# A two-layer graph network: order of the work inside a share, and a later load of the features

## The chip, the cores and the metric

The kernel runs on one core of a Trainium2 chip, as one launch. The metric is the device time of that launch in microseconds (us). A core has five engines with a queue each: TensorE (PE, matmuls), VectorE (DVE), ScalarE (ACT), GpSimd (POOL) and SyncE (SP). In this kernel SP issues the plain DMAs and POOL the indirect ones (gathers and scatters by a list of indices). Each queue is worked off in its order: an instruction that waits for a semaphore holds what stands behind it.

## The reference

There are 16 graphs (batches) of N = 1024 nodes with C = 64 features each; `adj` is a 0/1 matrix, symmetric, with about 16 neighbours in a row; every node is valid.

```
adj_d = dilate(adj, mask)                 # rows with over 10 neighbours drop every skip-th of them, symmetrically
agg   = weighted sum of the 0.25, 0.5 and 0.75 quantiles, per feature, over the neighbours kept
y     = relu((x + agg) @ W1 + b1) @ W2 + b2
x1    = layernorm(x + y * mask)           # layer 1
msg   = adj @ x1
out   = layernorm(x1 + tanh([x1, msg] @ W1' + b1') @ W2' + b2')    # layer 2
```

The quantiles need, for each node and feature, the sorted values of some 9 to 40 neighbours.

## The kernel before, in words

The batches are taken in five groups of 2, 4, 4, 4 and 2 (`GROUPS`). A group goes through four kinds of work.

**Preparation** (`prepare`, which runs `list_batch` for each batch, L610 to L714). For each half of a batch it loads four adjacency tiles `a` of 128 x 1024 (L620, three buffers), clears the diagonal (L621), loads the tile's features into the last columns of the tile `nb` (L623), turns the adjacency into 0/1 in the first columns of `nb` (L624) and counts it on ACT (L628). A second loop over the same four tiles transposes `nb` (L650, on PE), ranks the neighbours with matmuls (L656, L658) and marks those to drop (L660, L662). Then the kept neighbours of all eight tiles are computed back into `nb` (`p_val`, L670 to L675), the nodes are ordered by their number of neighbours (`places`, L681 to L704), and eight indirect DMAs on POOL scatter the eight tiles `nb`, neighbours and features in one row, into the DRAM tensor `order` (L708). `nb` has nine buffers (`held`, NT + 1), so that a new batch's tile needs a buffer whose scatter has landed.

**Fetch** (`Chunk.fill`, `ChunkByPE.fill`). A group's ordered nodes are cut into chunks of like degree: 9 or 10 for a group, 48 in all. For most chunks DVE finds the positions of the neighbours (MAX8, L817) and POOL gathers one neighbour's features a DMA (L837) into `slots_a` (three buffers). For the others, "by PE", the values come from matmuls with one-hot matrices `hot` that DVE makes (L976, L984), copied to `slots_a` by ACT (L995). Both put the nodes' own features there or into `x_n` first (L826, L925), and pads by ACT copies (L831).

**Selection** (`Chunk.select`). DVE runs a network of min and max over the slots (L873), ACT and PE weight the selected places (L895, L897), then come the first layer's matmuls and its layer norm (L544 to L552, of which ACT does the squares, L548), and the result goes to DRAM (`keep`, L853 or L1002).

**Second layer** (`finish_group`, which runs `messages` for each batch, L1013 to L1054). POOL gathers `x1` back into the order of the nodes (L1017); the adjacency is loaded again (L1025, the same three buffers `a`), transposed on PE (L1030) and copied by ACT (L1031); then come message matmuls (L1040) and the final layer norm.

The main loop (from L1091) runs over steps `s`, one for each chunk. The work of a step is handed out in 24 equal shares (`SHARES`): each kind of work is a Python generator wrapped in `Side`, and `advance` runs it on until its portion of the share is given out. `beside` lists the sides of a step: `fills` of chunk s + 1 (the second half of it) and of chunk s + 2 (the first half), `select` of chunk s, then `going` (the second layer of the group before) and `coming` (the preparation of the next group). At a group's first fetch, what is left of `coming` is drained in one piece. Steps before 0 hand out fills alone; the second layer of the last group is given out after the loop.

Waits, buffers and the final order of each engine's instructions come from the tile framework, which is given the written order. The order in the trace departs from the written one where an instruction was expected to be ready sooner.

Of the kernel before, what the change touches and what calls it, by code (L numbers as in the profile page):

```python
# [9 lines left out]
F32 = mybir.dt.float32  # L10
# [10 lines left out]
P = 128  # L21
# [395 lines left out]
def kernel(  # L417
# [15 lines left out]
    nc = tc.nc  # L433
# [5 lines left out]
    XCOL = N + 2 * INFO  # L439
# [170 lines left out]
    def list_batch(g, b):  # L610

        nbs, gone = [], []
        for half_b in range(2):
            at = slice(b * NT + half_b * HT, b * NT + (half_b + 1) * HT)

            m = rows.tile([P, 2, HT], F32, name="m")
            for t in range(half_b * HT, (half_b + 1) * HT):
                blk = slice(t * P, (t + 1) * P)
                a = rows.tile([P, N], F32, name="a", bufs=3)
                nc.sync.dma_start(a, adj[b, blk, :])  # L620
                nc.vector.tensor_mul(a[:, blk], a[:, blk], off_diag_f)  # L621
                nb = held.tile([P, ROW], BF16, name="nb")
                nc.sync.dma_start(nb[:, XCOL:].bitcast(F32), x[b, blk, :])  # L623
                nc.vector.tensor_scalar(nb[:, :N], a, 0.0, None, op0=ALU.is_gt)  # L624
                r = held.tile([P, N], BF16, name="gone", bufs=NT)
                for h in range(2):
                    cols = slice(h * HALF, (h + 1) * HALF)
                    nc.scalar.activation(r[:, cols], nb[:, cols], AF.Copy,  # L628
                                         accum_out=m[:, h, t - half_b * HT:t - half_b * HT + 1])
                nbs.append(nb)  # L630
                gone.append(r)
                yield


            s = rows.tile([P, 5, HT], F32, name="s")
            skip, do, want, biases = s[:, 0], s[:, 1], s[:, 2], (s[:, 3], s[:, 4])
            mh = halves[:, at]
            nc.vector.tensor_add(mh, m[:, 0], m[:, 1])
            nc.vector.tensor_scalar(mh, mh, 0.5, 0.25, op0=ALU.mult, op1=ALU.add)
            nc.vector.tensor_scalar(skip, mh, ROUND, -ROUND, op0=ALU.add, op1=ALU.add)  # L640
            nc.vector.scalar_tensor_tensor(do, mh, 0.5 * T_THRESH + 0.25, mask[:, at],
                                           op0=ALU.is_gt, op1=ALU.mult)
            nc.vector.scalar_tensor_tensor(want, skip, 1.0, do, op0=ALU.add, op1=ALU.mult)
            nc.vector.tensor_scalar(biases[0], skip, -3.0, -2.0 * FAR, op0=ALU.mult, op1=ALU.add)
            nc.vector.scalar_tensor_tensor(biases[1], m[:, 0], 2.0, biases[0], op0=ALU.mult, op1=ALU.add)
            for t in range(half_b * HT, (half_b + 1) * HT):
                nb, r, col = nbs[t], gone[t], slice(t - half_b * HT, t - half_b * HT + 1)
                p = ps_t.tile([P, N], BF16, name="p_nb", tag="tr")
                for j in range(NT):
                    nc.tensor.transpose(p[:, j * P:(j + 1) * P], nb[:, j * P:(j + 1) * P], ident_h)  # L650
                nb_t = rows.tile([P, N], BF16, name="nb_t")
                nc.scalar.copy(nb_t, p)  # L652

                for h in range(2):
                    p = ps_m.tile([P, HALF], F32, name="p_rank", tag="rv", bufs=3)
                    nc.tensor.matmul(p, far_h, nb[:, h * HALF:(h + 1) * HALF], start=True, stop=False)  # L656
                    for c in range(HT):
                        nc.tensor.matmul(p[:, c * P:], nb_t[:, (h * HT + c) * P:(h * HT + c + 1) * P],  # L658
                                         reach[:, :HALF - c * P], start=False, stop=c == HT - 1)
                    nc.scalar.activation(r[:, h * HALF:(h + 1) * HALF], p, AF.Abs,  # L660
                                         bias=biases[h][:, col], scale=2.0)
                nc.vector.tensor_scalar(r, r, 1.0, want[:, col], op0=ALU.add, op1=ALU.is_equal)  # L662
                yield
        count = work.tile([P, 2, NT], F32, name="count")
        for t in range(NT):
            blk = slice(t * P, (t + 1) * P)
            for h in range(2):
                cols = slice(h * HALF, (h + 1) * HALF)
                p = ps_m.tile([P, HALF], F32, name="p_val", tag="rv", bufs=3)
                nc.tensor.matmul(p, ident_h, nbs[t][:, cols], start=True, stop=False)  # L670
                nc.tensor.matmul(p, minus_h, gone[t][:, cols], start=False, stop=False)
                for j in range(HT):
                    nc.tensor.matmul(p[:, j * P:(j + 1) * P], gone[h * HT + j][:, blk], minus_h,
                                     start=False, stop=j == HT - 1)
                nc.scalar.activation(nbs[t][:, cols], p, AF.Relu, accum_out=count[:, h, t:t + 1])  # L675
            yield

        mine = work.tile([P, NT, INFO], F32, name="mine")
        nc.scalar.copy(mine[:, :, 1], mask[:, b * NT:(b + 1) * NT])
        deg = mine[:, :, 0]  # L680
        nc.vector.scalar_tensor_tensor(deg, count[:, 0], 1.0, count[:, 1], op0=ALU.add, op1=ALU.add)  # L681
        low = work.tile([P, NT], F32, name="low", bufs=1)
        nc.vector.tensor_scalar(low, deg, float(BINS - 1), None, op0=ALU.min)
        own = work.tile([P, NT, BINS], BF16, name="own", bufs=1)
        nc.vector.tensor_tensor(own, bins[:, None, :].to_broadcast([P, NT, BINS]), bcast(low, BINS),
                                op=ALU.is_equal)
        p = ps_m.tile([P, 512], F32, name="p_tot", tag="m")
        for t in range(NT):
            nc.tensor.matmul(p[:, :BINS], ones_h, own[:, t], start=t == 0, stop=t == NT - 1)
        base = work.tile([P, BINS + 1], F32, name="base", bufs=1)  # L690
        nc.vector.memset(base[:, 0:1], 0.0)
        nc.vector.tensor_tensor_scan(base[:, 1:], ones_h[:, :BINS], p[:, :BINS], 0.0, op0=ALU.mult, op1=ALU.add)
        p = ps_m.tile([P, NT, BINS], F32, name="p_at", tag="m")
        nc.tensor.matmul(p, ident, base[:, None, :BINS].to_broadcast([P, NT, BINS]), start=True, stop=False)
        for t in range(NT - 1):
            nc.tensor.matmul(p[:, t + 1:], ones_h, own[:, t:t + 1].to_broadcast([P, NT - 1 - t, BINS]),
                             start=False, stop=False)
        nc.tensor.matmul(p, above, own, start=False, stop=True)
        hit = work.tile([P, NT, BINS], F32, name="at_hit", tag="wide", bufs=1)
        nc.vector.tensor_mul(hit, p, own)  # L700
        at = work.tile([P, NT], F32, name="at", bufs=1)
        nc.vector.tensor_reduce(at, hit, AX.X, ALU.add)
        at_i = places[:, b * NT:(b + 1) * NT]
        nc.vector.tensor_copy(at_i, at)  # L704
        moves = []
        for t in range(NT):
            nc.vector.tensor_copy(nbs[t][:, N:XCOL].bitcast(F32), mine[:, t])
            move = nc.gpsimd.indirect_dma_start(  # L708
                out=g.order[b - g.b0], out_offset=bass.IndirectOffsetOnAxis(ap=at_i[:, t:t + 1], axis=0),
                in_=nbs[t].bitcast(I32), in_offset=None)  # L710
            for other in moves:
                tc.declare_no_dep(move.ins, other.ins, reason="the places of all nodes differ")
            moves.append(move)
        yield  # L714
# [378 lines left out]
    coming = start(0)  # L1093
    coming_of, going = 0, None
    fills = {}
    for s in range(-LEAD, len(plan)):
        j = s + LEAD
        if j < len(plan):
            i, (k, t0, t1, by_pe) = plan[j]
            if coming is not None and i == coming_of:  # L1100
                coming.drain()
                coming = start(i + 1) if i + 1 < len(GROUPS) else None
# [5 lines left out]
        beside = []  # L1108
# [5 lines left out]
        select = None  # L1114
        if s + 1 < len(plan) and (s < 0 or plan[s][0] != plan[s + 1][0]) and s + 1 >= 0:
            weigh_group(groups[plan[s + 1][0]])
        if s >= 0:
            i = plan[s][0]

            if s > 1 and plan[s - 1][0] == i != plan[s - 2][0] and i:  # L1120
                if going is not None:
                    going.drain()
                going = Side(finish_group(groups[i - 1]), groups[i - 1].count * (NT + NT // QT + 1))
            select = Side(chunks[s].select(), chunks[s].select_count())
# [4 lines left out]
            if coming is not None:  # L1129
                beside.append((coming, weight[min(s + LEAD, len(plan) - 1)] / sum(  # L1130
                    w for w, (q, _) in zip(weight, plan) if q == coming_of - 1)))
        for _ in range(SHARES):
            for side, share in beside:
                side.advance(share / SHARES)
# [220 lines left out]
```

## Time and profile before

| | |
|---|---|
| median of 3 runs | 3105.35 us (3076.01, 3105.35, 3121.26) |
| the profiled execution | 3108.18 us, span 3106.3 us |
| granted TensorE clock, mean | 0.891 |
| instructions | 65,859 |
| L837, fetches on POOL | 1012, 1412.1 us busy, mean 1395 ns |
| L873, selection on DVE, the three costliest groups of it | 355.4, 284.8 and 197.1 us |
| L984, `p_slots` on PE | 12,288 matmuls, 710.8 us, mean 270 ns |
| L976, `hot` on DVE | 456, 310.8 us, mean 697 ns |
| DMA | 264.06 MB, mean 85 GB/s |

The busy time of an engine leaves out waits, DMA issues and semaphore instructions. A list of waits says which instruction's engine stood idle before it, which instruction or DMA it waited for, for how long in total, how often and how long at most. "SPq" is SP's queue of DMA issues. "issue" stands for a time in which the engine waited for nothing that the profile shows. A timeline gives the start, the duration and the instruction, with the idle time before it and what ended it in brackets. The time of a DMA instruction on SP or POOL is that of its issue; the data land later.

### The profile page before, as it was taken

What the parts mean: (1) busy time and instruction counts of PE and PEld (TensorE: products, weight loads), DVE (VectorE), ACT (ScalarE), POOL (GpSimd) and SP (SyncE); (2) the same over time, 40 slices, a digit from 0 to 9 for tenths busy, and PEclk for the clock granted to TensorE, in tenths of its full rate; (3) what the DMA queues carried; (4) which work ended last, traced back from release to release, by engine and by line L of the source; (5) the groups of instructions that cost most, each with busy time, mean ns of one, the idle gap of its engine ahead of it and who ended that gap; (6) DMA issues with size and microseconds to landing.
All of it is one profiled execution on the core that took longest, in us unless ns stands there. A gap on an engine that the chain in (4) does not pass through costs nothing. (4 is left out here: it accounts for less than half of the span.)

```text
span 3106.3 us, 65859 instructions
## 1 busy us (share of the span) xinstructions
PE 2404.8 (77%) x25076; PEld 1875.9 (60%) x25076; DVE 2385.0 (77%) x5434; ACT 1593.3 (51%) x4047; POOL 1735.7 (56%) x1511
## 2 busy tenths in 40 slices
PE   5447847778577989885788999876868996689977
PEld 2245635466465777574566787664757875567755
DVE  3359957579579998997698978995898888967731
ACT  5615636646154656752356656633445455335553
POOL 3174762156856386638588465657552756646410
PEclk9769978889788999897899999997989998889988
DMA  2420332323132424241332424312421232122222
GB/s 96 146 76 24 113 105 92 104 59 113 41 119 55 122 57 121 67 127 40 105 82 75 135 72 122 97 43 56 125 82 50 70 102 76 43 68 80 70 87 80
DMA packets 223571, 264.06 MB, mean 85 GB/s; under 512 B 149683, under 2 KB 150290, under 8 KB 223248
## 3 DMA queue, kind: packets, MB, share of 16 engines
q1 hardware_dynamic: 176528, 189.18, 20.7%
q0 software_dynamic: 46720, 70.61, 8.8%
q8 instruction: 198, 3.24, 0.4%
q14 instruction: 125, 1.02, 0.1%
HBM read 218.07 MB, written 46.27 MB: 85 GB/s over the span
## 5 line engine op out<-in xcount | busy, mean ns | idle before, releaser
L837 POOL DMA_INDIRECT slots_a<-in_x_dram,idx x1012 | 1412.1, 1395 | 815.1 <-issue 270.9
L984 PE MATMUL p_slots<-hot,parts 128*64 128x256 bf16 (+1 forms) x12288 | 710.8, 270 | 182.3 <-DVE hot L976 156.5
L984 PEld LDWEIGHTS <-parts 128*64 128x64 bf16 x12288 | 636.7, 114 | 228.6 <-issue 109.8
L873 DVE TENSOR_TENSOR slots_b<-slots_a 128x256 f32<-128x256 f32 (+14 forms) x582 | 355.4, 627 | 101.9 <-DMA slots_a<-in_x_dram,idx 46.6
L1040 PE MATMUL p_msg<-adj_t,x_n 128*64 128x128 f32 x2048 | 281.3, 289 | 59.6 <-DMA x_n<-x,places 33.1
L976 DVE TENSOR_SCALAR hot<-val 128x2048 bf16<-128x2048 bf16 x456 | 310.8, 697 | 16.7 <-PE p_slots L984 8.9
L708 POOL DMA_INDIRECT order<-nb,places x128 | 149.6, 1169 | 307.8 <-issue 293.8
L897 PE MATMUL p_g<-ident,terms 128*64 128x128 f32 x1988 | 272.6, 288 | 30.1 <-ACT terms L895 29.4
L1040 PEld LDWEIGHTS p_msg<-adj_t,x_n 128*64 128x64 f32 x2048 | 233.2, 143 | 92.7 <-DMA x_n<-x,places 42.7
L873 DVE TENSOR_TENSOR slots_a<-slots_b 128x256 f32<-128x256 f32 (+11 forms) x526 | 284.8, 554 | 0.7
L995 ACT COPY slots_a<-p_slots 128x512 f32<-128x512 f32 (+2 forms) x136 | 73.2, 538 | 400.3 <-PE p_slots L984 288.1
L897 PEld LDWEIGHTS p_g<-ident,terms 128*64 128x64 f32 x1988 | 231.9, 144 | 57.4 <-ACT terms L895 47.4
L628 ACT ACTIVATE gone<-nb 128x512 bf16<-128x512 bf16 x256 | 159.8, 627 | 205.1 <-DVE nb L624 204.0
L1017 POOL DMA_INDIRECT x_n<-x,places x128 | 150.6, 1177 | 176.7 <-DMA x<-y 84.2
L658 PE MATMUL p_rank<-reach,nb_t 128*128 128x512 bf16 (+3 forms) x1024 | 191.0, 322 | 53.1 <-ACT nb_t L652 51.9
L1030 PE MATMUL p_adj<-ident,a 128*128 128x128 f32 x1024 | 185.0, 296 | 48.8 <-DMA a<-in_adj_dram 26.6
L817 DVE MAX8 key<-code 128x8 f16<-128x1024 f16 x170 | 207.2, 1219 | 1.7
L658 PEld LDWEIGHTS <-nb_t 128*128 128x128 bf16 x1024 | 95.7, 104 | 178.6 <-ACT nb_t L652 91.3
L873 DVE TENSOR_TENSOR slots_b<-slots_b 128x256 f32<-128x256 f32 (+11 forms) x310 | 197.1, 636 | 0.6
L660 ACT ACTIVATE gone<-p_rank,s 128x512 bf16<-128x512 f32 x256 | 164.5, 685 | 56.7 <-PE p_rank L658 37.2
L624 DVE TENSOR_SCALAR nb<-a 128x1024 bf16<-128x1024 f32 x128 | 88.5, 692 | 132.7 <-DMA order<-nb,places 132.1
L1031 ACT COPY adj_t<-p_adj 128x512 f32<-128x512 f32 x256 | 149.1, 583 | 73.9 <-PE p_adj L1030 71.7
(184 smaller groups left out, 4551.2 us busy)
## 6 DMA issues: line engine op xcount, KB each, us to landing
a<-in_adj_dram SPq DMA_DIRECT2D x256, 512.0 KB
row_p<-order SPq DMA_DIRECT2D x64, 256.0 KB
slots_a<-in_x_dram,idx POOLq DMA_INDIRECT x1012
row<-order SPq DMA_DIRECT2D x192, 64.0 KB
nb<-in_x_dram SPq DMA_DIRECT2D x128, 32.0 KB
row<-order SPq DMA_DIRECT2D x32, 128.0 KB
x_s<-in_x_dram SPq DMA_DIRECT2D x16, 256.0 KB
out_dram<-x_n SPq DMA_DIRECT2D x16, 256.0 KB
```

The source lines that it names most:

```text
L628: nc.scalar.activation(r[:, cols], nb[:, cols], AF.Copy, accum_out=m[:, h, t - half_b * HT:t - half_b * HT + 1])
L658: nc.tensor.matmul(p[:, c * P:], nb_t[:, (h * HT + c) * P:(h * HT + c + 1) * P], reach[:, :HALF - c * P], start=False, stop=c == HT - 1)
L660: nc.scalar.activation(r[:, h * HALF:(h + 1) * HALF], p, AF.Abs, bias=biases[h][:, col], scale=2.0)
L817: nc.vector.max(key[:, t, r:r + 8], code)
L837: nc.gpsimd.indirect_dma_start(out=self.a[:, at[k], t, :], out_offset=None, in_=x_rows, in_offset=bass.IndirectOffsetOnAxis(ap=idx[:, t, k ...
L873: nc.vector.tensor_tensor(view(rb, ra, [(d[0], d[1 + side]) for d in dims]), view(ab, aa, [(d[0], d[1]) for d in dims]), view(bb, ba, [(d[ ...
L897: nc.tensor.matmul(p[:C, col], terms[:, i], ident, start=False, stop=t == e - 1 and first + i == places - 1)
L976: nc.vector.tensor_scalar(hot[:, :, :, e], val, float(inside[at]), None, op0=ALU.is_equal)
L984: nc.tensor.matmul(p[i * C:(i + 1) * C, o:o + w], g.parts[2 * q + i][:, c, h], hot[:, c, i, :w], start=c == 0 and h == 0, stop=c == NT - 1 ...
L1017: nc.gpsimd.indirect_dma_start(out=x1[:, t], out_offset=None, in_=g.x1[b - g.b0], in_offset=bass.IndirectOffsetOnAxis(ap=places[:, b * NT ...
L1030: nc.tensor.transpose(p[:, j, :], a[:, col:col + P], ident)
L1040: nc.tensor.matmul(p[C:2 * C, :QUART], x1[:, j, :], adj_t[:, j, :], start=(j == 0), stop=(j == NT - 1))
```

## The change

Two edits.

The load of a tile's features into `nb` moves within `list_batch` from the first loop over the four tiles of a half (between the load of `a` and the 0/1 adjacency) to the top of the second loop over the same tiles. It is the same DMA, of the same rows, into the same columns, on the same queue.

The list `beside` is sorted, once for each step, before its shares are handed out: first `going` and `coming`, then `select`, then the two `fills`. The sort is stable, so that within each of these the order stays. The portions of each side and the drains stay as they are.

```diff
@@ list_batch, first loop
                 nc.sync.dma_start(a, adj[b, blk, :])
                 nc.vector.tensor_mul(a[:, blk], a[:, blk], off_diag_f)
                 nb = held.tile([P, ROW], BF16, name="nb")
-                nc.sync.dma_start(nb[:, XCOL:].bitcast(F32), x[b, blk, :])
                 nc.vector.tensor_scalar(nb[:, :N], a, 0.0, None, op0=ALU.is_gt)
@@ list_batch, second loop
             for t in range(half_b * HT, (half_b + 1) * HT):
                 nb, r, col = nbs[t], gone[t], slice(t - half_b * HT, t - half_b * HT + 1)
+                nc.sync.dma_start(nb[:, XCOL:].bitcast(F32), x[b, t * P:(t + 1) * P, :])
                 p = ps_t.tile([P, N], BF16, name="p_nb", tag="tr")
@@ main loop
+        beside.sort(key=lambda b: (b[0] is not going and b[0] is not coming, b[0] is not select))
         for _ in range(SHARES):
             for side, share in beside:
                 side.advance(share / SHARES)
```

## The prediction

> **What bounds the kernel now.** I read the page first, for the balance of the engines:
>
> ```profile
> PE 2404.8 (77%) x25076; PEld 1875.9 (60%) x25076; DVE 2385.0 (77%) x5434; ACT 1593.3 (51%) x4047; POOL 1735.7 (56%) x1511
> ```
>
> TensorE and VectorE are each busy for 77%, so neither is the bound by itself; each loses about 700 us, and an order of work is worth what it takes out of those losses. The chain of waits on the page names only the code after the last batch and says nothing of the stages. The windows by stage do:
>
> ```profile
> 130.00:480.00 350.00, 211.92 (x2335) 161.30 (x2337) 265.04 (x735) 149.67 (x375) 209.93 (x150) 0.80 0.30 85
> 480.00:600.00 120.00, 97.64 (x863) 63.15 (x859) 65.77 (x180) 83.38 (x221) 26.42 (x24) 0.89 0.34 106
> 600.00:1500.00 900.00, 696.41 (x7652) 540.91 (x7651) 761.85 (x1679) 471.26 (x1198) 568.51 (x407) 0.88 0.30 84
> 3000.00:3106.00 106.00, 83.84 (x545) 63.57 (x545) 15.12 (x29) 44.16 (x107) 14.29 (x16) 0.91 0.30 93
> ```
>
> Columns: stretch, length, then busy time of PE, weight loads, DVE, ACT, POOL. From 600 to 1500 us DVE is busy for 85%; its idle time lies in the start, in 480 to 600 (the rest of group 1's preparation, given out in one piece: the shares of steps 0 to 5 hold weights 32+38+30+36+26+10 = 172 of group 0's 269, so 36% is drained) and after 3000 (the second layer of the last group, given out after the loop). None of these three is ordered by shares, so the new order can't help there.
>
> Next the waits, of the SP queue and of DVE:
>
> ```profile
> SPq L1025 <- PE p_adj L1030: 367.7, 69, 36.3
> SPq L623 <- DMA order<-nb,places: 366.5, 75, 39.4
> DVE nb L624 <- DMA order<-nb,places: 132.1, 31, 30.1
> DVE a L621 <- DMA a<-in_adj_dram: 65.3, 34, 8.6
> DVE slots_b L873 <- DMA slots_a<-in_x_dram,idx: 46.6, 5, 26.9
> ```
>
> (us in total, times, longest.) SP stands 366.5 us before the feature load of L623, for a buffer `nb` that the scatter of the batch before still reads. DVE waits for the same scatters itself at L624, which the change leaves as it is. The timelines of the turn at 860 us, POOL, SP and DVE, show how it hangs together:
>
> ```profile
> 845.78 1.00 POOL L837 DMA_INDIRECT slots_a<-in_x_dram,idx  x1 [0.31 <-issue]
> 847.08 0.96 POOL L1017 DMA_INDIRECT x_n<-x,places  x1 [0.30 <-issue]
> ...
> 857.10 1.01 POOL L708 DMA_INDIRECT order<-nb,places  x1 [0.30 <-DMA x_n<-x,places]
> ```
>
> ```profile
> 818.86 1.71 SPq L853 DMA_DIRECT2D x<-y  x4
> 860.06 10.21 SPq L623 DMA_DIRECT2D nb<-in_x_dram  x7
> 870.38 0.38 SPq L620 DMA_DIRECT2D a<-in_adj_dram  x1
> ```
>
> ```profile
> 860.01 0.69 DVE L624 TENSOR_SCALAR nb<-a 128x1024 bf16<-128x1024 f32 x1 [15.41 <-DMA order<-nb,places]
> ...
> 874.13 0.29 DVE L621 TENSOR_TENSOR a<-a,off_diag_f 128x128 f32<-128x128 f32 x1 [6.54 <-DMA a<-in_adj_dram]
> ```
>
> The batch's `places` were done at 836.2 (DVE timeline), but POOL first works off fetches, then eight gathers of the second layer, and only at 857.1 the scatters. DVE stands 15.4 us. Then SP hands out seven feature loads at the pace of the scatters, and the adjacency load behind them leaves at 870.4 instead of about 860.7, when L624 had freed its buffer: DVE stands another 6.5 us. The same sequence shows at 410, 1507 and 2151; the four turns cost DVE 30.9+15.8+14.3+29.1 = 90.1 us at L624.
>
> **What the Trainium skill says.** "DMA: Bandwidth & Descriptors", section "Anatomy of one DMA — SWDGE (gpsimd) path", says that DMA engines do not wait on semaphores, the issuing sequencer does, and that some 2 us of such a DMA are fixed, mostly the write receipt. The trace agrees with the first (SP's 39.4 us before one load), and nearly with the second: from the scatter's start at 857.10 to L624 at 860.01 are 2.9 us. "SBUF — State Buffer", section "SBUF: two separate sides", says that POOL can't write descriptors while DVE holds the shared port in a fast mode. A fetch at 840.12 took 5.35 us (median of the line 1.07) while DVE ran `hot` and `select`; this fits and isn't proof. So POOL's pace may move with DVE's order, which I can't price.
>
> **The change, part by part.** Nothing is added or removed: 128 feature loads, 1245 SP issues, 1268 indirect DMAs stay. A step between two stores of `y` takes (2996.6 - 289.4)/47 = 57.6 us, so a share is 57.6/24 = 2.4 us: nothing moves by more than about a share in written order.
>
> *Does written order count?* Only among instructions that are ready. In the tile view of `slots_a`:
>
> ```profile
> L831 ACT COPY slots_a<-big x214: 227/251/486, 30.5 to 2914.7; 128x64 f32<-128x64 f32 x65, 128x192 f32<-128x192 f32 x27, 128x128 f32<-128x128 f32 x12, 128x320 f32<-128x320 f32 x3
> L826 SPq DMA_DIRECT2D slots_a<-order x92: 313/427/1125, 91.3 to 2911.2; - x92
> ```
>
> L831 is written after L826, yet starts 61 us ahead: instructions are laid out by when they were expected to be ready, and written order breaks ties. That limits both edits.
>
> *Feature loads.* 128 x (0.34 + 0.05) us = 50 us of SP time stay on SP. A load needs only a free buffer, and may well be laid out as early as before: then nothing changes. At best every late adjacency load goes: 65.3 us at L621 less 4.0 in the first 60 us = 61. No loss of note: the 340 ns slot only moves past `a`, `row` and `x<-y` on SP, and the scatter that reads the features follows eight tiles of `p_val` later. I take a quarter, -15 us.
>
> *Preparation and second layer first.* On POOL the scatters (L708) and gathers (L1017) pass the fetches of their share: 1012 fetches over 48 x 24 shares are 0.88, each (1412.1 + 270.9)/1012 = 1.66 us, so 1.5 us, at most 2.4, per turn. Over 14 turns that is 20 to 34 us earlier, on DVE's path where it waited: I take -20. On DVE L621, L624 and L662 pass `hot`, MAX8 and `select`; an L624 placed a share earlier before a scatter that is late anyway stands longer, at worst 14 x 2.4 = 34 us. I take +5. What is queued behind it on DVE is the `select` of L873, and PE waits for `hot`.
>
> *Fetches last.* They are delayed by what is given out before them in their share. `select` waits for fetches in 5 places, 46.6 us; a share more each is 12 us, and it can't be below zero as the queue only gets fuller ahead of them; but if all 48 steps came to wait, 48 x 2.4 = 115 us. `hot` (L976, a fetch in the PE variant) is waited for by PE 52 times, 156.5 us; that can move either way by 52 x 2.4 = 125 us at the very most, and mostly other PE work fills in: 0. I take +0 for `hot`, +0 for steps that have slack, and the turns' small loss above stands for both.
>
> Sum: -15 - 20 + 5 = -30 us. The profiled execution took 3108.2 (span 3106.3, 2 us around it), the median of three is 3105.4 (3076.0 to 3121.3), so the profiled one is as good as the median: 3075.
>
> **The rivals.**
> *A, as summed (chance 0.42):* 3075, own range 3040 to 3115. That the feature loads don't move at all lies in it (3090).
>
> *B, faster (0.34):* the turns open up. If the scatters pass not one share's fetches but the whole run in front of them (13 after 833 us at the turn above; 27 in a row before the scatters of 437), two thirds of the 90.1 us at L624 go, 60, and with SP free two thirds of the 61 at L621, 41: 3105 - 101 = 3004. For it: POOL is 56% busy, so it could well serve them earlier. Against: the scatters look to have been laid out for a time at which POOL was expected to be done with the fetches, and then rank is no matter. What is late next is DVE's wait for ACT's squares (L549, 126.6 us), which stays.
>
> *C, slower (0.24):* the fetch of the next chunk becomes the bound. It used to be handed out first in each share, so it had the rest of the share as slack before the first `select`; now it comes last. Add to that POOL's queue: a scatter ahead of fetches holds them while it waits (L708 already stands 293.8 us on POOL). If two thirds of the 48 steps pay a share, 77 us: 3182. It decides from the point at which the waits of L873 for `slots_a` pass about 80 us, from 46.6.
>
> **How the numbers follow.** A measurement of this kernel can tell about 2%, some 62 us (the three runs before differ by 45). Faster by over 2% means under 3043: most of B (0.31) and a little of A (0.05), 0.36. Slower means over 3167: most of C (0.20) and a rest, 0.21. Within 2%: 0.43. The likeliest is A, so 3075. For 8 in 10 the range reaches to the middle of B and past that of C: 2975 to 3190.
>
> **What would show it.** Right: SP's wait at L623's load (now in the second loop) falls from 366.5 us to under 100, with part of it coming back at L620 for a buffer of `a`; L621's 65.3 falls by a quarter or more; L624's 132.1 falls by about 20; L873's wait for fetches rises by 5 to 15; the windows before 130, 480 to 600 and after 3000 stay within a few us. If SP's wait for the scatters stays near 366, the features are laid out as before and that part is nothing. The sum is wrong if L624's wait falls by half or more (B), if L873's wait for fetches or PE's for `hot` rises by over 30 us (C), or if waits that I left at zero, L549's for ACT above all, move by tens of us because the layout comes out different everywhere.

## The result, and the profile after

The changed kernel took 3064.89 us (median of four, 3051.81 to 3070.3) beside 3107.37 for the kernel before (3076.01 to 3121.26): a ratio of 0.9878, 95% interval 0.9831 to 0.9925. Its profiled execution spans 3068.3 us, 38.0 less than the one before. Measured again in the second series below it came to 0.9846 [0.982, 0.9872]. A ratio leaves out executions that took over 1.5% longer than the fastest of the same kernel.

The balance of the engines on the page after:

```profile
PE 2410.6 (79%) x25076; PEld 1897.4 (62%) x25076; DVE 2383.7 (78%) x5434; ACT 1594.5 (52%) x4047; POOL 1737.3 (57%) x1511
```

The counts of instructions and DVE's 2384 us of work are those of before, so the gain is idle time alone. The list of waits after (us in total, times, longest), with the features' load now on L647 and the 0/1 step on L623:

```profile
ACT gone L627 <- DVE nb L623: 213.8, 55, 37.7
ACT node_t L1042 <- PE p_msg L1040: 177.0, 99, 9.1
DVE nb L623 <- DMA order<-nb,places: 151.5, 32, 36.9
...
DVE ln_st L549 <- ACT ln_sq L548: 80.3, 35, 12.5
...
DVE a L621 <- DMA a<-in_adj_dram: 52.0, 31, 7.4
...
PE p_msg L1040 <- ACT adj_t L1031: 38.2, 3, 35.7
...
DVE slots_b L873 <- DMA slots_a<-in_x_dram,idx: 34.7, 3, 24.8
...
PE p_msg L1040 <- DMA x_n<-x,places: 7.6, 8, 1.9
...
PE p_x L1036 <- DMA x_n<-x,places: 1.7, 1, 1.7
```

and four lines of the list of before that the prediction had not shown:

```profile
ACT node_t L1042 <- PE p_msg L1040: 193.7, 102, 27.5
...
DVE ln_st L549 <- ACT ln_sq L548: 126.6, 34, 26.0
...
PE p_msg L1040 <- DMA x_n<-x,places: 33.1, 24, 16.8
...
PE p_x L1036 <- DMA x_n<-x,places: 20.4, 2, 18.6
```

The wait for the scatters, for which the prediction saw a fall, rose from 132.1 to 151.5 us (138.4 in the repeat, `e5_full_again`). What fell is a wait that it had left at zero: DVE's for ACT's squares at L549, by 46.3, and with it PE's waits for gathered rows `x_n`, from 53.5 to 9.3. The longest of each (26.0, 16.8, 18.6, and 27.5 on ACT) shrank too: a few long stops went, not many short ones.

SP, in its own list of the kernel after:

```profile
SPq L647 <- DMA order<-nb,places: 330.8, 45, 50.3
...
SPq L620 <- DVE nb L623: 59.3, 33, 10.0
```

SP still stands 330.8 us at the feature load (366.5 before). DVE's work in the stage of group 1's drained preparation and at the end is as it was (the windows after give DVE 67.39 us busy from 480 to 600, 65.77 before, and 15.13 in the last 106 us, 15.12 before).

**Where the 38 us are.** DVE's stops of over 10 us add up to 292.6 us before and 254.7 after, a difference of 37.9, as much as the span lost. In the repeat they add up to 241.4, 51.2 less than before, and its span is 49.8 shorter. All of the 37.9 lies at the four turns from one group to the next:

| stops of DVE at the turn (us) | before | after | the changed kernel again |
|---|---|---|---|
| first, from 404 to 410 | 30.2 (L624) | 11.0 | 10.9 |
| second, from 791 to 802 | 23.7 (L549) and 15.4 (L624) | 24.1 (L623) | 24.2 |
| third, from 1431 to 1453 | 26.0 (L549) and 14.1 (L624) | 36.9 (L623) | 24.1 |
| fourth, from 2089 to 2151 | 29.1 (L624) | 28.6 | 27.3 |
| sum | 138.5 | 100.6 | 86.5 |

At the second and third turn two stops became one. The timeline of the kernel before shows how the first of such a pair came about (start, duration, engine and instruction; in brackets the idle time before it and what ended that):

```profile
789.66 0.22 DVE L546 TENSOR_TENSOR y<-y,ln_st 128x64 f32<-128x64 f32 x1
...
794.96 0.99 POOL L837 DMA_INDIRECT slots_a<-in_x_dram,idx  x1 [0.30 <-issue]
796.26 0.96 POOL L1017 DMA_INDIRECT x_n<-x,places  x1 [0.31 <-issue]
...
798.84 0.69 PE L1040 MATMUL p_msg<-adj_t,x_n 128*64 128x128 f32 x2 [16.83 <-DMA x_n<-x,places]
...
801.28 0.94 POOL L1017 DMA_INDIRECT x_n<-x,places  x1 [0.30 <-issue]
802.53 1.01 POOL L837 DMA_INDIRECT slots_a<-in_x_dram,idx  x1 [0.30 <-issue]
...
804.40 0.26 ACT L1042 COPY node_t<-p_msg 64x128 f32<-64x128 f32 x1 [27.52 <-PE p_msg L1040]
...
814.44 0.25 ACT L548 ACTIVATE ln_sq<-y 128x64 f32<-128x64 f32 x1
...
814.72 0.22 DVE L549 TENSOR_REDUCE ln_st<-ln_sq 128x1 f32<-128x64 f32 x1 [23.70 <-ACT ln_sq L548]
```

POOL had given out three gathers of the second layer at 722 to 725 us, then 33 fetches, and came to the next five gathers at 796.26. PE stood 16.8 us before the message matmuls for the first of these; ACT stood 27.5 for the message to copy; the squares of a layer norm of *selection*, whose input `y` DVE had finished at 789.9, stood behind that copy on ACT's queue, and behind 10 us of other ACT work that came next on it (some of it waiting for PE in its turn); DVE stood 23.7 for the squares. While POOL was busy with fetches, the gathers behind them held PE, ACT and DVE one after the other, and the wait list puts it down to ACT.

After the change, the same place:

```profile
812.85 1.00 POOL L837 DMA_INDIRECT slots_a<-in_x_dram,idx  x1 [0.30 <-issue]
814.15 0.96 POOL L1017 DMA_INDIRECT x_n<-x,places  x1 [0.30 <-DMA slots_a<-in_x_dram,idx]
...
820.41 1.01 POOL L708 DMA_INDIRECT order<-nb,places  x1 [0.30 <-DMA x_n<-x,places]
...
823.33 0.69 DVE L623 TENSOR_SCALAR nb<-a 128x1024 bf16<-128x1024 f32 x1 [24.06 <-DMA order<-nb,places]
823.44 0.35 SPq L647 DMA_DIRECT2D nb<-in_x_dram  x1
824.05 0.33 SPq L620 DMA_DIRECT2D a<-in_adj_dram  x1
```

Eleven gathers ran from 692.44 us on, ahead of all fetches; PE no longer stands. Then 62 fetches follow in one run, five gathers, and only then the scatters, and DVE stands 24.1 us for them. The scatters left at 857.1 before and leave at 820.4 now, yet DVE reaches them earlier too, so its wait for them grew. The adjacency load behind the feature load leaves 0.6 us after it, where it took 10 us before: seven features no longer stand ahead of it.

At the third turn of the changed kernel a chain runs the other way, and it is the longest stop left: DVE stands 36.9 us at L623 for the scatters, ACT stands 37.7 at L627 for DVE's 0/1 tile, the adjacency copy of L1031 comes behind that on ACT's queue, and PE stands 35.7 at L1040 for the copy.

### The profile page after: what moved, and what is told of

The parts are those of the page before. It is cut to its first block, busy times and chain, and to the rows that moved or that the text cites. A ratio compares the mean times of both kernels' runs of the same rounds, so it can differ in the third digit from the quotient of the medians.

```text
span 3068.3 us, 65888 instructions
## 1 busy us (share of the span) xinstructions
PE 2410.6 (79%) x25076; PEld 1897.4 (62%) x25076; DVE 2383.7 (78%) x5434; ACT 1594.5 (52%) x4047; POOL 1737.3 (57%) x1511
## 5 line engine op out<-in xcount | busy, mean ns | idle before, releaser
L837 POOL DMA_INDIRECT slots_a<-in_x_dram,idx x1012 | 1383.5, 1367 | 762.3 <-issue 287.1
L984 PE MATMUL p_slots<-hot,parts 128*64 128x256 bf16 (+1 forms) x12288 | 720.5, 273 | 145.2 <-DVE hot L976 135.1
L984 PEld LDWEIGHTS <-parts 128*64 128x64 bf16 x12288 | 649.2, 115 | 193.1 <-issue 130.9
L873 DVE TENSOR_TENSOR slots_b<-slots_a 128x256 f32<-128x256 f32 (+14 forms) x582 | 355.1, 628 | 91.4 <-ACT terms L895 37.1
L1040 PE MATMUL p_msg<-adj_t,x_n 128*64 128x128 f32 x2048 | 281.9, 292 | 61.3 <-ACT adj_t L1031 38.2
L708 POOL DMA_INDIRECT order<-nb,places x128 | 158.6, 1239 | 292.1 <-issue 257.7
L1040 PEld LDWEIGHTS p_msg<-adj_t,x_n 128*64 128x64 f32 x2048 | 239.4, 146 | 88.6 <-ACT adj_t L1031 39.1
L1017 POOL DMA_INDIRECT x_n<-x,places x128 | 171.7, 1342 | 205.9 <-DMA x<-y 85.5
L873 DVE TENSOR_TENSOR slots_a<-slots_b 128x256 f32<-128x256 f32 (+11 forms) x526 | 286.0, 556 | 0.7
L627 ACT ACTIVATE gone<-nb 128x512 bf16<-128x512 bf16 x256 | 160.0, 629 | 214.3 <-DVE nb L623 213.8
L1030 PE MATMUL p_adj<-ident,a 128*128 128x128 f32 x1024 | 186.0, 298 | 30.2 <-ACT adj_t L1031 16.4
L623 DVE TENSOR_SCALAR nb<-a 128x1024 bf16<-128x1024 f32 x128 | 88.8, 695 | 152.1 <-DMA order<-nb,places 151.5
L873 DVE TENSOR_TENSOR slots_b<-slots_b 128x256 f32<-128x256 f32 (+11 forms) x310 | 197.6, 638 | 0.5
L660 ACT ACTIVATE gone<-p_rank,s 128x512 bf16<-128x512 f32 x256 | 165.6, 685 | 48.3 <-PE p_rank L658 33.1
L1031 ACT COPY adj_t<-p_adj 128x512 f32<-128x512 f32 x256 | 148.9, 582 | 74.5 <-PE p_adj L1030 71.9
```

Of the source, the lines that this page charges most:

```text
L627: nc.scalar.activation(r[:, cols], nb[:, cols], AF.Copy, accum_out=m[:, h, t - half_b * HT:t - half_b * HT + 1])
L837: nc.gpsimd.indirect_dma_start(out=self.a[:, at[k], t, :], out_offset=None, in_=x_rows, in_offset=bass.IndirectOffsetOnAxis(ap=idx[:, t, k ...
L873: nc.vector.tensor_tensor(view(rb, ra, [(d[0], d[1 + side]) for d in dims]), view(ab, aa, [(d[0], d[1]) for d in dims]), view(bb, ba, [(d[ ...
L984: nc.tensor.matmul(p[i * C:(i + 1) * C, o:o + w], g.parts[2 * q + i][:, c, h], hot[:, c, i, :w], start=c == 0 and h == 0, stop=c == NT - 1 ...
L1017: nc.gpsimd.indirect_dma_start(out=x1[:, t], out_offset=None, in_=g.x1[b - g.b0], in_offset=bass.IndirectOffsetOnAxis(ap=places[:, b * NT ...
L1030: nc.tensor.transpose(p[:, j, :], a[:, col:col + P], ident)
```

## The experiments

The theory from the two traces is the chain above: gathers of the second layer that stood behind a run of fetches cost the time, and the sort let them pass. Its rivals: the features' later load did it through SP; it was the scatters of the preparation that passed fetches, as the prediction had it; or any change of order lands a layout that is faster or slower by chance. The expectations name these as they were called at the time: R (order by readiness, with the gain in the sort) and then G (the gathers) for the theory, F for the features, S for the preparation or the selection, P and L for chance.

All are edits of the kernel before. Each series ran on one chip. Two series fell on chips on which the kernel before took 3877.74 and 3885.52 us at a granted TensorE clock of 0.81; the second ran on one like that of the result (3108.22 us, 0.89). Ratios are taken within a series, and absolute times are compared there only.

### First series (clock 0.81): the two parts, and the order turned round

The features alone (`e1_features_only`: the two lines of the diff in `list_batch`), the sort alone (`e2_order_only`), and two other orders:

```diff
# e3_fetch_before_select: fetches ahead of selection, second layer and preparation still first
+        beside.sort(key=lambda b: (b[0] is not going and b[0] is not coming, b[0] is select))
# e4_select_first: selection, fetches, then second layer and preparation
+        beside.sort(key=lambda b: (b[0] is going or b[0] is coming, b[0] is not select))
```

> Only the move of the feature load; the shares are handed out as before. Theory R (instructions are laid out by readiness; a feature load needs only a free buffer, so the move is worth little, and the sort gives the gain): ratio to before 0.993 to 1.003, SP's wait for the scatters at the feature load stays over 250 us. Rival F (the feature load held SP, and its move gives the gain): ratio 0.983 to 0.991, DVE's wait for adjacency at L621 falls from 65 us to about 50. Theory P (any change of the written order lays the work out anew, and the time moves by up to 1% either way without a cause in the edit): anything from 0.985 to 1.015.

> Only the sort of the shares (second layer and preparation, then selection, then fetches); the feature load stays in the first loop. Theory R: ratio 0.984 to 0.992, nearly all of the gain, and DVE's wait for ACT's squares at L549 falls from 127 us to about 80 as in the changed kernel. Rival F: 0.996 to 1.004. Theory P: anything from 0.985 to 1.015, and not the sum that e1 and the full change would give.

> Feature load in the first loop; second layer and preparation first, then the fetches, then selection. Tells which half of the sort matters. If the gain lies in putting second layer and preparation first: as e2, ratio 0.984 to 0.993. If it lies in selection ahead of the fetches (the squares of its layer norm pass the ACT copies of the fetch by PE): 0.996 to 1.004, with L549's wait near 127 us. Theory P: anything from 0.985 to 1.015.

> Feature load in the first loop; selection first, then the fetches, then second layer and preparation. The other half of the sort alone. If the gain lies in selection ahead of the fetches: ratio 0.984 to 0.993 and L549's wait near 80 us. If it lies in second layer and preparation first: 0.996 to 1.004. Theory P: anything from 0.985 to 1.015.

Measured: 0.9992 [0.995, 1.0035], 0.998 [0.9953, 1.0006], 0.9982 [0.9956, 1.0009] and 1.0113 [1.0054, 1.0173]. On this chip neither part is worth anything that can be told; e2 so misses the 0.984 to 0.992 of theory R. Giving selection and fetches ahead of the rest costs about 1%, of which the clock may be a third: e4's executions had a mean of 0.8065 beside 0.8124, and a straight line through those of the kernel before that the ratio counts falls by 27.5 us for 0.01, an estimate of 16 of the 44 us. The list of waits of e1 shows a different balance:

```profile
PEld L984 <- issue: 450.7, 500, 3.6
...
PE p_slots L984 <- issue: 301.9, 335, 3.5
```

PE stands some 300 us between its own matmuls where nothing that the profile shows holds it, and the span is 740 us longer. And PE waits for `x_n` not at all in e1. There, in the list of one line's instructions (times in ns least/median/most, then first and last start in us), the gathers

```profile
L1017 POOL DMA_INDIRECT x_n<-x,places x128: 938/945/9057, 890.7 to 3773.5; - x128
```

begin at 890.7, and the first matmul that reads them (L1036) at 965.5: POOL has 75 us. So this series can't show the gain of gathers that come earlier, as they are never late. It shows something else, which is used below: the order of POOL's instructions.

### Second series (clock 0.89): the same parts, and the features held back

The changed kernel again (`e5_full_again`), the features alone (`e6_features_again`), the sort alone (`e7_order_again`), and the changed kernel with one word of the feature columns set by DVE after the 0/1 step, so that the feature load can't be laid out ahead of it:

```diff
# e8_features_forced, beside both edits of the change
                 nc.vector.tensor_scalar(nb[:, :N], a, 0.0, None, op0=ALU.is_gt)
+                nc.vector.memset(nb[:, XCOL:XCOL + 2].bitcast(F32), 0.0)
```

> The full change again, for a comparison with its parts on one chip. The parts were timed on a chip whose TensorE is granted 0.81 of its clock (before: 3878 us there), and gave 0.999 and 0.998. If this run's chip is like that one (before near 3880): theory R and theory P expect 0.993 to 1.003, since TensorE's own pace is more of the bound there; rival F expects the sum of the parts, 0.997. If the chip is like the first one (before near 3107): 0.984 to 0.992.

> The move of the feature load alone, again, beside the full change. Theory R: 0.995 to 1.003. Rival F: as the full change, within 0.003. Theory P: different from its first measurement only through the chip, and without relation to the full change.

> The sort alone, again, beside the full change. Theory R: within 0.004 of the full change. Rival F: 0.996 to 1.004.

> The full change, and DVE clears one word of the feature columns right after the 0/1 adjacency, so that a tile's feature load can't be laid out ahead of that tile's 0/1 step: SP never stands at a feature load for a scatter again. It adds 128 DVE memsets of some 60 ns, 8 us. Theory R: DVE stands at the 0/1 step for the same scatter anyway, so SP's freedom is worth at most what DVE waits for adjacency (52 us at L621 in the changed kernel): 0.99 to 1.002 of the full change. Rival F: the feature load is what costs, and 0.98 or less of the full change.

Measured: full 0.9846 [0.982, 0.9872] (3060.09 us); features 0.9974 [0.9956, 0.9993] (3100.65); sort 0.9911 [0.9884, 0.9938] (3079.31); features forced 0.9887 [0.986, 0.9914] (3070.42). e5 and e6 fall where theory R had them; e7 is 0.0065 from the full change, where R allowed 0.004, and e8 is 1.0035 of it, just above R's range.

The sort is the larger part, 28 us; the features give 8. Together they give 48, some 12 more than their sum, with an uncertainty of about 9. The clock may have a share here too: the means were 0.8952 (full), 0.8932 (features) and 0.8912 (sort) beside 0.8913 before, and a straight line through the 23 of the kernel before falls by 23.6 us for 0.01. By this estimate 9 us of the full change's gain and 4 of the features' go with the clock, and none of the sort's. Waits of e6, features alone:

```profile
DVE nb L623 <- DMA order<-nb,places: 132.9, 35, 30.6
...
DVE ln_st L549 <- ACT ln_sq L548: 107.7, 34, 19.5
...
PE p_x L1036 <- DMA x_n<-x,places: 27.2, 3, 15.8
```

and of e7, the sort alone:

```profile
DVE nb L624 <- DMA order<-nb,places: 140.3, 33, 30.5
DVE ln_st L549 <- ACT ln_sq L548: 86.6, 33, 13.0
...
PE p_msg L1040 <- DMA x_n<-x,places: 10.9, 11, 1.9
PE p_x L1036 <- DMA x_n<-x,places: 1.3, 1, 1.3
```

The sort alone takes away PE's waits for `x_n` (12.2 us are left of 53.5) and 40 of the 46 us at L549; the features alone leave 41.3 and take 19, and both long stops of DVE at L549 are still there (18.0 and 19.5 us, 23.7 and 26.0 before). Of the 12 us that only the pair brings, one place is visible: with the sort alone DVE stops for 15.8 us at 998.8 before L624, which in the changed kernel is under 10. Why it goes is not shown.

e8 bounds the features' best case. SP's wait for scatters at the feature load fell to 7.7 us, but SP now stands at the adjacency load, for DVE (L624 is here the added word, just behind the 0/1 step that reads the buffer). SP's list of e8:

```profile
SPq L620 <- DVE nb L624: 155.1, 12, 36.0
```

DVE's wait for adjacency fell to 29.9 us, and the kernel is no faster than the changed one (0.9887 beside 0.9846). POOL's order in it is, but for one fetch, that of the sort alone (table below), and against e7 it is 9 us faster, though the intervals overlap: a queue of SP that is free of this wait is worth about what the features gave in e6, not the 61 us of the prediction's upper bound.

### Third series (clock 0.81 again): which place in the order does it

```diff
# e9_second_layer_first: second layer, fetches, selection, preparation
+        beside.sort(key=lambda b: going is None or b[0] is not going)
# e10_preparation_first: preparation, fetches, selection, second layer
+        beside.sort(key=lambda b: coming is None or b[0] is not coming)
# e11_preparation_then_second: beside both edits, preparation, second layer, selection, fetches
+        beside.sort(key=lambda b: (b[0] is not coming, b[0] is not going, b[0] is not select))
# e12_25_shares
-    SHARES = 24
+    SHARES = 25
```

> Only the second layer is put first in each share; fills, selection and preparation keep their order, the features load where they did. Theory G (the cost was the gathers of L1017 standing on POOL behind a run of fetches, which held PE, then ACT's node_t copy, then the squares of L548, then DVE): 0.985 to 0.994 of the kernel before; PE's waits for x_n (L1036 and L1040 together, 53.5 us before) fall under 20, DVE's wait for the squares at L549 (126.6) falls by 25 or more. Rival S (it was the preparation put first, or selection put ahead of fetches): 0.996 to 1.004. Theory L (any change of order lands a layout at random): anything from 0.985 to 1.015, without a tie to the x_n waits.

> Only the preparation is put first in each share; the rest keeps its order. Theory G: 0.996 to 1.004, PE's waits for x_n stay near 53 us. Rival S, in its form with the preparation: 0.985 to 0.993 and DVE's waits for scatters (L624, 132.1 us before) fall by 20 or more. Theory L: anything from 0.985 to 1.015.

> The changed kernel with the preparation ahead of the second layer in the sort, so that of one share the scatters of L708 are given out ahead of the gathers of L1017. If the scatters pass the gathers: DVE's waits for scatters (L623 and L624, 151.5 us in the changed kernel) fall by some 30 and the ratio is 0.975 to 0.985. If the gathers come late for PE again: x_n waits over 30 us and 0.990 to 1.000. If the two hardly meet in one share: the changed kernel's 0.985 to 0.988.

> The kernel before with SHARES = 25 in place of 24: a control that keeps the order within a share and only shifts every boundary. Theory G: 0.996 to 1.004, with x_n waits of 40 us or more; should the gathers happen to come out ahead of the fetches, those waits fall and the time with them. Theory L: anything from 0.985 to 1.015 while the x_n waits stay.

Measured: 0.9827 [0.9742, 0.9911], 0.9935 [0.9897, 0.9973], 0.9996 [0.9958, 1.0035] and 1.0016 [0.9979, 1.0052]. The control stays at one. e11 gains nothing here, so no order better than the changed one was found. None of these four could be timed where gathers are late.

e9 came out a little faster than the 0.985 to 0.994 expected of it, and not for the expected reason. PE waits for no `x_n` in e12's list of waits either, so there was none to lose, and DVE's wait at L549 is no lower than elsewhere on such chips (e1 had 63.9):

```profile
DVE ln_st L549 <- ACT ln_sq L548: 160.7, 31, 46.1
```

That profiled execution, 3846.93 us, was the slowest of e9's six (3770.3 to 3846.93). The other five had a mean clock of 0.8192, the 34 of the kernel before that the ratio counts 0.8125; a straight line through those 34 falls by 48.8 us for 0.01 of clock, which puts 33 us of the 75 between the means to the clock. Whether the order brought the clock, and where the other 42 us come from, stays open. e10 gained 0.65% with a mean clock of 0.8173, which by the same line is all of its 24 us.

### POOL's order, read across all kernels

What can be read on any chip is the order of one engine's instructions. The same kernel has the same order on both kinds of chip (e1 and e6; e2 and e7). Below, F, G and S are fetches (L837), gathers (L1017) and scatters (L708) in POOL's order, taken from the traces; "3G 33F 5G" is three gathers, then 33 fetches, then five gathers. "First turn" is the fetches ahead of the third run of scatters, of 75; "second" and "third" are what stands between the scatters there.

| kernel (order in a share) | first turn | second turn | third turn | ratio, clock 0.89 |
|---|---|---|---|---|
| before (F, select, G, preparation) | 65 | 3G 33F 5G 29F 8G | 33F 8G 29F 8G | 1 |
| e6 (the same, features later) | 63 | 33F 8G 29F 8G | 33F 8G 29F 8G | 0.9974 |
| e12 (25 shares) | 66 | 30F 8G 32F 8G | 30F 8G 32F 8G | - |
| e9 (G first) | 65 | 3G 30F 5G 32F 8G | 30F 8G 32F 8G | - |
| e10 (preparation first) | 50 | 33F 8G 29F 8G | 33F 8G 29F 8G | - |
| e3 (G and preparation, F, select) | 50 | 30F 8G 32F 8G | 30F 8G 32F 8G | - |
| e4 (select, F, G, preparation) | 66 | 13G 62F 3G | 33F 8G 29F 8G | - |
| e7 (G and preparation, select, F) | 50 | 16G 62F | 30F 8G 32F 8G | 0.9911 |
| e8 (the same, features forced) | 49 | 16G 62F | 30F 8G 32F 8G | 0.9887 |
| e11 (preparation, then G, select, F, features later) | 50 | 11G 62F 5G | 30F 8G 32F 8G | - |
| after, e5 | 50 | 11G 62F 5G | 8G 62F 8G | 0.9878, 0.9846 |

Two separate effects. **The preparation first** lets the scatters of the first turn pass 15 fetches: 49 or 50 instead of 65 stand ahead in e3, e7, e8, e10, e11 and after, and in none of the others. That is the first row of the table of stops. Before:

```profile
435.62 1.00 POOL L837 DMA_INDIRECT slots_a<-in_x_dram,idx  x1 [0.30 <-issue]
436.92 1.03 POOL L708 DMA_INDIRECT order<-nb,places  x1 [0.30 <-issue]
...
439.90 0.69 DVE L624 TENSOR_SCALAR nb<-a 128x1024 bf16<-128x1024 f32 x1 [30.15 <-DMA order<-nb,places]
```

After:

```profile
411.78 1.02 POOL L708 DMA_INDIRECT order<-nb,places  x1 [0.30 <-DMA slots_a<-in_x_dram,idx]
...
414.83 0.69 DVE L623 TENSOR_SCALAR nb<-a 128x1024 bf16<-128x1024 f32 x1 [11.02 <-DMA order<-nb,places]
```

15 fetches at 1.3 us from one to the next are 19.5 us; DVE's stop fell by 19.1. The count of fetches isn't all of it: in e6, with 63 ahead, the stop is 21.3. But the chips with the lower clock bear the link out: there this stop is 22.4 to 31.8 us in e1, e4, e9 and e12, and under 10 in e2, e3 and e10 and 13.0 in e11, which put the preparation first. That it shrank didn't by itself make those kernels faster (e2 0.998, e3 0.9982, e11 0.9996).

**Selection ahead of the fetches** lets the gathers of the second turn pass the whole run: e4, e7, e8, e11 and after have 11 to 16 gathers ahead of every fetch, all others three at most. Putting the second layer first without it (e9, e3) does not do it. Why it takes selection is argued and not shown: a gather needs `x` from DRAM, where `keep` puts it at the end of selection, and with the fetches given out first that store is expected later. At the third turn gathers went ahead of the whole run only in the changed kernel; with the sort alone they come after 30 of the fetches there, and yet PE waits little for them: they leave POOL from 1408 us on there, 49 us earlier than before. This second effect is a reading of orders: what it is worth in time was measured only together with the first, in e7.

So both the theory and the rival with the scatters have their place, at different turns; how the sort's 28 us divide between them is open. The chain of late gathers is seen at 796 to 815 us before, and is gone in after, e5 and e7, where they pass the run; that the second layer's own place in the share moved them, as e9 was meant to show, fell. The features as a cause are bounded by e6 and e8. Chance isn't excluded on the chips with the lower clock, where e9 and e10 gained without a late gather; e12 and e11 speak against it there. At 0.89, where gathers are late, no control such as e12 was timed, so how far a chance layout moves the time there isn't known. What speaks for a cause there is that the stops of DVE that went account for the time, in both traces of the changed kernel.

## Why the prediction was right or wrong

The time was right: 3075 forecast, 3064.89 measured, inside case A's own range. The mechanism was right in part only. By the prediction's own sign the sum was wrong, for L549's wait, left at zero, moved by tens of us; and SP's wait at the feature load, which was to fall under 100 us, hardly moved. By its terms:

- **Feature loads, -15.** Measured alone -8.1 us (0.26%, interval 2 to 14). The doubt stated there was the right one: SP's wait stayed at 330.8 of 366.5. L621's wait fell by 13.3 of 65.3, near the quarter forecast, but it fell as far with the sort alone (50.6 in e7) and by 5.6 with the features alone (59.7 in e6). The upper bound of 61 fell with e8, where the loads were held back and some 9 came of it.
- **Preparation and second layer first, -20.** The size was near (the sort alone gave -28, with the next term in it), the working was not. It took a share's 0.88 fetches, 1.5 us, at each of 14 turns. Its ground for small moves was weak: L831 and L826 stand on different queues (ACT and SP), so that one starts 61 us ahead says nothing of the order within a queue. The 27 fetches in a row before the scatters of 437, in rival B, are those from 395 us on; the run has 65. POOL's order moved by runs: 15 fetches at one turn (-19 us on DVE), and a run of 33 or more that gathers passed at the next. And it costed the gathers only as something ahead of the scatters, not as what PE waits for.
- **The wait at L624, "falls by about 20".** Failed. It fell by 19 at the first turn and rose by 31 at the second and third together (by 19 in the repeat), since DVE arrives there sooner once the gather stops are gone and a group's last gathers and a run of 62 fetches still stand ahead of the scatters. The +5 for DVE's earlier placing was thus too small, and mis-named: not an L624 placed a share early, but a stop of another kind removed just ahead of it.
- **L549, left at zero.** This is the step that failed. The page and the waits of PE for `x_n` (33.1 and 20.4 us, longest 16.8 and 18.6) were there to be read; rival B named L549 as what "stays". It fell by 46.3, and it was the second layer's gathers that it hung on.
- **Fetches last, 0, and L873's wait "rises by 5 to 15".** It fell, 46.6 to 34.7. Rival C, fetches as the bound, set in at 80 us; in the runs at a clock of 0.89 this wait is 31.8 to 50.2. 24.8 us of the 34.7 are one stop near 183 us, ahead of the shares that matter.
- **`hot`, 0.** PE's wait for it went from 156.5 to 135.1, within what was said of it.
- **Windows outside the shares.** DVE's busy time as forecast, within 2 us; PE's from 480 to 600 fell from 97.6 to 87.8.

So that the sum came out near was luck: a gain left out (L549, 46 us) stood in for one forecast in the wrong place (L624, a fall of 20 that turned into a rise of 19, or of 6 in the repeat).

## What to carry to other kernels

When one in-order queue serves two consumers, list it in runs, not in averages: which instruction stands at the end of a run of the other kind, and who waits for it. Follow a long wait on one engine (here DVE for ACT's squares) back through the queues, instruction by instruction, until it reaches a DMA: the engine named in the list had only been standing behind something else. And where two stops follow one another closely, taking one away lengthens the other; count the pair.

## What the runs showed of the hardware

- The same kernel took 3107, 3878 or 3886 us by the chip it ran on, with clocks of 0.89 and 0.81. In e1 PE's busy time was 9% higher (2625 us, 2405 before) and it stood 300 us before L984 without a named cause, a wait that the list of before does not have. The sort's gain of 0.9% at 0.89 was 0.2% [-0.06, 0.47] at 0.81, where PE never waits long for a gather.
- A fetch takes POOL 1.00 us (median) when DVE is idle at its start, and none of 186 takes over 1.9. When DVE is in one of L873's longest operations (TENSOR_TENSOR of some 128x2048 f32, 2.02 to 2.36 us, two inputs) 20 of 24 do, median 2.16, and all 24 end 0.87 to 0.92 us after that operation does; beside MAX8 (1.22 us, one input) none of 49 takes over 1.9. "SBUF — State Buffer", section "SBUF: two separate sides", of the Trainium skill says that DVE and POOL share a port pair that one instruction holds for its whole length, and counts a DVE operation with two SBUF inputs among those that do, against a POOL operation that reads SBUF. These counts, from the trace of the kernel before, agree with it; that a fetch reads its indices from SBUF at that point is not shown. The prediction had named only the fast modes. Its fetch of 5.35 us at 840.12 ends at 845.47, 0.87 us after DVE's run of L873 and `hot` ends and DVE stands still (844.60). So a network of min and max on DVE slows the very fetches that feed its next chunk.
